# Layer 2's windows: another order of ScalarE's instructions, and other clearing at an image's beginning

## The chip, the cores and the metric

The kernel runs on one core of one Trainium2 chip. The metric is device time in microseconds (us) of one execution, told as the median of several runs. Engines are named as the profile names them: PE is TensorE (matrix products and transposes), DVE is VectorE, ACT is ScalarE, POOL is GpSimd, SP is SyncE, which here only issues transfers (DMAs). DVE and ACT can read PSUM, the memory that PE writes; POOL works on SBUF alone. Each engine runs its own instructions in order and waits on semaphores for those of others.

## The reference, cut to what matters

Four layers follow each other on a batch of 4 images of 192 channels and 64 x 64 pixels in float32. Layer 0 is a deformable convolution with channel attention and an MLP, layer 1 a non-local block, layer 2 attention in overlapping windows with a gated MLP, layer 3 a depthwise convolution with weights computed from the image. The change is in layer 2's attention:

```python
y = _conv1x1(_ln_c(x, n1g, n1b), qkv_w, qkv_b)
cols = _unfold(y, WS, STRIDE, PAD)          # windows of 8 x 8, 6 apart, image padded by 3 zeros
...
q = win[:, :, :HEADS] * temp[None, None]
k = win[:, :, HEADS:2 * HEADS]
v = win[:, :, 2 * HEADS:]
attn = jnp.einsum('blhic,blhjc->blhij', q, k)
attn = attn + bias[None, None]
e = jnp.exp(attn - jnp.max(attn, axis=-1, keepdims=True))
s = jnp.sum(e, axis=-1, keepdims=True)
s_img = _reverse(s, H, W)                   # overlapping windows are added up
o = jnp.einsum('blhij,blhjc->blhic', e, v)
o_img = _reverse(o, H, W).reshape(B, HEADS, ch, H, W)
out = (o_img / s_img[:, :, None]).reshape(B, C, H, W)
```

There are 11 x 11 windows an image and 6 heads of 32 channels. `_ln_c` is a layer norm over the channels of each pixel. The padding makes rows and columns of zeros around the projected image.

## The kernel before, in words

The whole kernel is one program that works image by image. After layer 1 of image b has written its output to the DRAM tensor `x_flat` (tile `xd`, L1050), the function `windows(b, ...)` (from L1095) makes the divided attention output `oi` of that image; `rest` then does the remainder of layers 2 and 3.

**Rows.** `windows` walks over 11 rows of windows (`wr`). For each row it projects a strip of 6 image rows (4 in the last), which are the rows that this row of windows adds to those it shares with the row before. Its work on a row `wr` is woven with the preparation of the next ones:

- `load` (L1118, L1119) brings a strip of `x_flat` into one of two tiles `xr`, in two DMAs: 128 channels, and 64 channels into the lower half of a second block whose upper half is zero.
- `norm_steps` (L1163 to L1179) is the layer norm, as a generator that can be stopped after a step: the squares on ACT (L1163, step SQUARE); the means on PE (tile `pv`, L1170), a square on ACT (L435), a difference and a maximum with zero on DVE (L436, L437), then a logarithm and an exponential on ACT (L398, L399, step INVERSE) for the inverse root; spreading it on PE (`pb`, L427) and scaling the strip on DVE (`xz`, L1179).
- `project_rows(wr, t)` (L1203) makes queries and keys of a strip in three parts t, in a PSUM tile of tag "a", which ACT copies out: t = 0 into `qs` (L1212), t = 1 into `ks` (L1209), t = 2 in halves into both (L1212, L1216). `qs` and `ks` are padded tiles, two sets of them used in turn; `shared` (L1191, POOL) copies the rows that two rows of windows share from one set to the other.
- `values` (L1231, L1235) projects the values in two parts through tag "a" and DVE, and SP writes them to the DRAM tensor `values_dram` (L1243); `fetch` (L1253) reads them back by windows with 16 DMAs on SP into `vw`.
- `queries` (L1264 to L1266) gathers the windows' queries into `qw` on POOL.

**Groups.** The 11 windows of a row are worked on in three groups `g` of four, four and three. `scores` (L1279) makes the scores of a group in the one PSUM tile `s`, and DVE adds the bias (L1285); `lowered` takes the maximum (L1295) and subtracts it (L1296), both on DVE; `exponentials` (L1300) is one ACT instruction of 128 x 768; `summed` (L1306, L1310) makes the sums on DVE. A group has two pairs of windows. `turned` transposes a pair's exponentials on PE (tile `t`, tag "a", L1325) and ACT copies them into `et` (L1329, two copies, one where the pair has only one window). `outputs` multiplies them with the values (L1345) and gathers the sums (L1353) in the PSUM tile `o`; `collect` (L1363, L1364, ACT) copies that out once a row. `inverses` (L1384, L1385, ACT) makes 1/sum of the row before by logarithm and exponential, and `finish` spreads it on PE (`rb`, tag "a", L1390) and multiplies on DVE into `oi` (L1391), in two halves.

**What sets the order.** This stage is written under `tc.manual_schedule()`: each engine gets its instructions in the order of the program text, from L1400 on. PE's order in a full row is, for g = 0: scores of g = 1, t, o, qk (t = 0), v, t, o, qk (t = 2), v; for g = 1: scores of g = 2, t, o, qk (t = 1), t, o, pv; for g = 2: scores of the next row's g = 0, t, o, rb, pb, t, o, rb. The exponentials of the next group are asked for after both pairs of the group and, in g = 1, after the norm's INVERSE step:

```python
                        if wr + 2 < NWIN and g == 1:
                            norm(wr + 2, INVERSE)
                        if nxt[0] < NWIN:
                            ex = exponentials(*nxt, sc)
```

Tag "a" has two PSUM buffers, handed out in turn, for t, qk, v and rb alike: each tile waits until the one two before it has been read. DVE's order in g = 2 is: bias sum of the next row, sums L1306, maximum, subtraction, first `oi`, `xz`, second `oi`.

**An image's beginning.** POOL clears the upper halves of both `xr` (L1124), issues the first two loads (four DMAs), clears the four tiles `qs` and `ks` whole (L1136, 128 x 1224 each), three tiles `et` (L1141) and two tiles `rs` (L1154); for image 0 also a tile `blank` (L1145), from which six DMAs on POOL's queue write the zero border of `values_dram` (L1147 to L1150). The order of text is: square of the first norm, `keep_warm` (matmuls whose result nobody reads, L788), the load of ACT's table for logarithms and exponentials (`table(LN_EXP)`, L393), the rest of the norm, the three projections, queries, values, second norm, fetch, and then the first scores.

`constants` (L261) holds one more line of the change: a copy of a small PSUM tile `wide` (128 x 52), once in the program.

Of the kernel before, what the change touches and what calls it, by code (L numbers as in the profile page):

```python
# [10 lines left out]
F32 = mybir.dt.float32  # L11
# [7 lines left out]
B, C, H, W = 4, 192, 64, 64  # L19
# [5 lines left out]
M, Q = 128, 64  # L25
# [31 lines left out]
NWIN = 11  # L57
# [24 lines left out]
def conv_seq_kernel(ctx: ExitStack, tc: tile.TileContext, a, out: bass.AP):  # L82
    nc = tc.nc
# [102 lines left out]
    def constants():  # L186
# [59 lines left out]
        with pool_of(name="wideps", bufs=1, space=PSUM) as pp:  # L246
            n = sum(n for name, n in _V96 if name in _WIDE)
            wide = const([M, 2, n], "wide")
            p = pp.tile([M, 2, n], F32, tag="p", name="p_wide")
            at = 0  # L250
            for name, n in _V96:
                if name in _WIDE:
                    cols = slice(at, at + n)
                    at += n
                    for to, of, k in (
                        (p[0:P, 0, cols], slice(0, P), 0), (p[P:M, 0, cols], slice(0, M - P), 1),
                        (p[0:Q, 1, cols], slice(M - P, P), 1), (p[Q:M, 1, cols], slice(M - P, P), 1),
                    ):
                        nc.tensor.matmul(to, lhsT=ident[:P, of], rhs=V[name][:, k, :], start=True, stop=True)
                    VW[name] = wide[:, :, cols]  # L260
            nc.vector.tensor_copy(wide, p)  # L261
        yield
        fc1_dram, fc1_bias = folded("fc1", V["l0_g2"], V["l0_b2"], V["l0_bfc1"])
        yield
# [113 lines left out]

    xn_flat = [dram.tile([C, XNW], F32, tag=f"xnd{i}", name=f"xnd{i}") for i in range(2)]
    x_flat = [dram.tile([C, HW], F32, tag=f"xd{i}", name=f"xd{i}") for i in range(2)]  # L380
    values_dram = dram.tile([SW, STRIDE * (NWIN + 1), C], F32, tag="values", name="values")
    xn_drams, x_drams = ([t.rearrange("(k p) n -> p k n", p=P) for t in ts] for ts in (xn_flat, x_flat))

    in_order = []
# [707 lines left out]
                beside(None)  # L1092


    def windows(b, oi, load_image):  # L1095


        inside = slice(PAD, PAD + W)
        with ExitStack() as s:
# [14 lines left out]
            def load(wr, by=nc.sync):  # L1114
                n, at = strip(wr)
                t = given[wr] = xrs[wr % 2]
                lo, hi = split(t, n)
                by.dma_start(out=lo, in_=x_flat[b % 2][0:M, at : at + n])  # L1118
                by.dma_start(out=hi[half(0)], in_=x_flat[b % 2][M:C, at : at + n])  # L1119

            xrs = []
            for j in range(2):
                xr = s1.tile([M, 2, STRIDE * W], F32, tag=f"xr{j}", name=f"xr{j}_{b}")
                nc.gpsimd.memset(xr[half(1), 1, :], 0.0)  # L1124
                xrs.append(xr)

            load(0, nc.gpsimd)
            load(1, nc.gpsimd)


            sets = []
            for j in range(2):
                qs = s1.tile([M, 2, WS + 1, SW], F32, tag=f"qs{j}", name=f"qs{j}_{b}")
                ks = s1.tile([M, 2, WS + 1, SW], F32, tag=f"ks{j}", name=f"ks{j}_{b}")
                for t in (qs, ks):
                    nc.gpsimd.memset(t, 0.0)  # L1136
                sets.append((qs, ks))
            ets = []
            for j in range(3):
                et = s1.tile([128, 3, 2, WS, WS + STRIDE], F32, tag=f"et{j}", name=f"et{j}_{b}")  # L1140
# [2 lines left out]
            if b == 0:  # L1143
                blank = s1.tile([128, 3 * C], F32, tag="blank", name="blank")
                nc.gpsimd.memset(blank, 0.0)  # L1145
                for r in (0, 1, 2, SW - 1):
                    nc.gpsimd.dma_start(out=values_dram[r, 0:SW], in_=blank[0:SW, 0:C])  # L1147
                inner = values_dram[PAD : PAD + H]
                nc.gpsimd.dma_start(out=inner[:, 0:PAD, :], in_=blank[0:H].rearrange("p (w c) -> p w c", c=C))
                nc.gpsimd.dma_start(out=inner[:, PAD + W, :], in_=blank[0:H, 0:C])  # L1150
            rss = []
            for j in range(2):
                rs = s1.tile([128, 512], F32, tag=f"rs{j}", name=f"rs{j}_{b}")
# [27 lines left out]
            def norm(wr, upto=None):  # L1181

                if wr not in norms:
                    norms[wr] = norm_steps(wr)
                links(norms[wr], upto)

            def shared(wr, i):

                to, of = sets[wr % 2][i], sets[1 - wr % 2][i]
                if wr > 0:  # L1190
                    nc.gpsimd.tensor_copy(to[:, :, 0:PAD, :], of[:, :, STRIDE : STRIDE + PAD, :])  # L1191
                end = PAD + strip(wr)[0] // W
                if end < WS + 1:
                    nc.gpsimd.memset(to[:, :, end : WS + 1, :], 0.0)
# [204 lines left out]
            groups = -(-NWIN // WG)  # L1399
            with tc.manual_schedule():  # L1400
                warm = ps2.tile([128, 512], F32, tag="a", name=f"warm_{b}")[:, 0:384]
                norm(0, SQUARE)
                keep_warm(warm, 2)
                in_order.append(None)
                table(LN_EXP)
                norm(0, VARIANCE)
                keep_warm(warm, 2)
                norm(0)
                keep_warm(warm, 1)
                for t in range(3):  # L1410
                    project_rows(0, t)
                    if t == 0:
                        norm(1, SQUARE)
                queries(0)
                norm(1, VARIANCE)
                values(0, 0)
                values(0, 1)
                norm(1)
                fetch(0)
                load(2)  # L1420
                ex, top = scores(0, 0)
                lowered(0, 0, ex, top)
                exponentials(0, 0, ex)
                due = None
                for wr in range(NWIN):
                    for g in range(groups):
                        nxt = (wr, g + 1) if g + 1 < groups else (wr + 1, 0)
                        if nxt[0] < NWIN:
                            sc, top = scores(*nxt)
                        sums = summed(wr, g, ex)  # L1430
                        if nxt[0] < NWIN and (g > 0 or wr + 1 == NWIN):
                            lowered(*nxt, sc, top)
                        if wr + 3 < NWIN and g == 1:
                            load(wr + 3)
                        for pair in range(WG // 2):
                            ops = turned(wr, g, pair, (ex, sums))
                            if due is not None:
                                outputs(*due)
                                if g == 0 and pair == 0:
                                    collect(wr - 1)  # L1440
                            due = ops
                            if wr + 1 < NWIN:
                                if g == 0:
                                    project_rows(wr + 1, 2 * pair)
                                    values(wr + 1, pair)
                                if g == 1 and pair == 0:
                                    project_rows(wr + 1, 1)
                                if g == 0 and pair == 0:
                                    lowered(*nxt, sc, top)
                            if wr == 0 and g == 0 and pair == 0:  # L1450
                                norm(2, SQUARE)
                            if wr > 0 and g == 1 and pair == 0:
                                inverses(wr - 1)
                            if wr > 0 and g == 2:
                                finish(wr - 1, pair)
                            if wr + 2 < NWIN and g == 2 and pair == 0:
                                norm(wr + 2)
                        if wr + 2 < NWIN and g == 1:
                            norm(wr + 2, INVERSE)
                        if nxt[0] < NWIN:  # L1460
                            ex = exponentials(*nxt, sc)
                        if wr + 3 < NWIN and g == 2:
                            norm(wr + 3, SQUARE)
                        if wr + 1 < NWIN:
                            if g == 0:
                                shared(wr + 1, 0)
                                queries(wr + 1)
                            if g == 1:
                                shared(wr + 1, 1)
                                fetch(wr + 1)  # L1470
                    if wr == 1:
                        load_image()
                outputs(*due)
                collect(NWIN - 1)
                inverses(NWIN - 1)
                keep_warm(ps2.tile([128, 512], F32, tag="a", name=f"warm2_{b}")[:, 0:384], 4)
                for h in range(2):
                    finish(NWIN - 1, h)
                in_order.pop()
# [35 lines left out]
    def half(h):  # L1515
        return slice(Q * h, Q * h + Q)
# [697 lines left out]
```

## Time and profile before

| | |
|---|---|
| median of 21 runs | 6435.1 us (6414.39 to 6451.02) |
| the profiled execution's own time | 6434.07 us |
| span of its profile | 6432.3 us |
| mean granted clock of PE | 0.946 |
| PE busy | 5833.2 us (91%) |
| DVE busy | 4645.4 us (72%) |
| ACT busy | 3720.7 us (58%) |
| POOL busy | 1982.5 us (31%) |

All times are of one profiled execution, in us from the span's start. Lines of a timeline give start, duration, engine, line (L and the line number of the kernel), the operation, the tile that it writes and those that it reads (written<-read), shapes, and in square brackets how long the engine was idle just before and what ended that. Lines of the chain of waits give start, duration and the piece of work; "issue" is time in which an engine waited for nothing that the profile shows. Lines of stretches give from:to, length, then the busy time and number of instructions of PE, PE's weight loads, DVE, ACT and POOL, then the granted clock of PE as a share of full speed, the busy share of the DMA engines and what they moved in GB/s.

### The profile page before, as it was taken

The numbers are of one execution on the slowest core, as the hardware profiler recorded it, in microseconds if no ns is written. First come the engines' busy times: TensorE is split into PE (matmuls) and PEld (weight loads), VectorE is DVE, ScalarE is ACT, GpSimd is POOL, SyncE is SP. The second block draws the span as 40 slices with busy tenths as digits, with TensorE's granted clock in tenths as the row PEclk, the third lists the DMA queues.
The fourth block names the chain that finished last, engine by engine and source line by source line (L and its number), as shares of the span: only waits on it lengthen the run. The fifth ranks groups of instructions, "written<-read, shape, count | busy, mean of one in ns | idle before, by whom it ended". The sixth has DMA issues, their size and how long they took to land.

```text
span 6432.3 us, 105494 instructions
## 1 busy us (share of the span) xinstructions
PE 5833.2 (91%) x39860; PEld 4021.9 (63%) x39860; DVE 4645.4 (72%) x6899; ACT 3720.7 (58%) x6288; POOL 1982.5 (31%) x1989
## 2 busy tenths in 40 slices
PE   8887999998879899999888899999888989998897
PEld 4555688886544468887554458888654457775443
DVE  3764189985677659996676849998567867766667
ACT  3764378874545358885654438887455536545542
POOL 2764067751100037772110007775110000001100
PEclk8889999999889899999999999999988999998898
DMA  6986267762110266773210047775221020002100
GB/s 180 294 298 184 71 191 225 224 189 61 46 45 16 62 187 212 231 220 91 78 48 26 19 129 229 223 223 177 62 51 34 16 64 10 13 15 70 28 8 22
DMA packets 385632, 735.33 MB, mean 114 GB/s; under 512 B 67757, under 2 KB 272189, under 8 KB 384358
## 3 DMA queue, kind: packets, MB, share of 16 engines
q0 software_dynamic: 93264, 455.82, 22.0%
q1 hardware_dynamic: 291030, 271.99, 15.6%
q8 instruction: 316, 5.18, 0.3%
q14 instruction: 190, 1.56, 0.1%
q10 hardware_dynamic: 832, 0.79, 0.0%
HBM read 635.04 MB, written 91.86 MB: 113 GB/s over the span
## 4 chain that ended last, share of the span: by engine, by line
PE 63%; DVE 19%; ACT 8%; DMA 4%; issue 4%; SPq 1%; POOL 1%; DVEq 0%; ACTq 0%; POOLq 0%
PE y L1076 11%; PE s L1008 10%; PE h L685 7%; PE qk L1203 3%; DVE ha L1507 2%; PE h L1699 2%; PE o L913 2%; PE po L573 2%; DMA ring<-table,idx 2%; DVE ga L1507 2%; PE t L1325 2%; DVE gate L1507 1%; PE o L1345 1%; PE rb L1390 1%; DVE row L674 1%
## 5 line engine op out<-in xcount | busy, mean ns | idle before, releaser
L667 POOL DMA_INDIRECT ring<-table,idx x1152 | 1659.6, 1441 | 967.8 <-DVE row L674 175.6
L1008 PE MATMUL s<-ths,ph 96*128 96x256 f32 x4096 | 982.5, 381 | 6.9 <-ACT sc L1010 4.6
L1008 PEld LDWEIGHTS s<-ths,ph 96*128 96x128 f32 x4096 | 777.0, 191 | 130.6 <-ACT sc L1010 6.2
L673 ACT ACTIVATE row<-ring,pos 128x384 f32<-128x384 f32 x1152 | 672.5, 608 | 243.1 <-DVE xo L678 143.7
L674 DVE SCALAR_TENSOR_TENSOR row<-ring,fr,row 128x384 f32<-128x384 f32 x1152 | 674.9, 614 | 114.6 <-ACT row L673 109.5
L1076 PE MATMUL y<-sc,gx 128*97 128x256 f32 x3008 | 716.4, 379 | 0.0
L1076 PEld LDWEIGHTS y<-sc,gx 128*97 128x97 f32 x3008 | 489.3, 164 | 127.5 <-issue 5.1
L677 ACT ACTIVATE xo<-row,pos 128x192 f32<-128x192 f32 x1152 | 486.3, 448 | 72.8 <-PE h L685 34.6
L678 DVE SCALAR_TENSOR_TENSOR xo<-row,fr,xo 128x192 f32<-128x192 f32 x1152 | 448.2, 414 | 45.1 <-ACT xo L677 42.6
L1010 ACT COPY sc<-s 128x1024 f32<-128x1024 f32 x376 | 377.3, 1004 | 157.4 <-PE s L1008 154.5
L1073 DVE TENSOR_TENSOR sc<-sc,mbs 128x1024 f32<-128x1024 f32 x376 | 453.9, 1220 | 19.9 <-ACT mbs L1034 19.8
L1015 DVE TENSOR_TENSOR top<-top,sc 128x1024 f32<-128x1024 f32 x282 | 344.6, 1222 | 128.1 <-ACT sc L1010 128.0
L1074 ACT ACTIVATE sc<-sc 128x1024 f32<-128x1024 f32 x376 | 393.3, 1053 | 75.1 <-DVE sc L1073 72.0
L685 PE MATMUL h<-ti,xo 128*128 128x192 f32 x2304 | 434.6, 327 | 0.0
L685 PEld LDWEIGHTS h<-ti,xo 128*128 128x128 f32 x2304 | 388.8, 190 | 28.8 <-issue 8.2
L1329 ACT COPY et<-t 64x384 f32<-64x384 f32 x484 | 231.7, 479 | 254.0 <-PE t L1325 249.0
L1507 DVE SCALAR_TENSOR_TENSOR ga<-gate,v,ga 128x1024 f32<-128x1024 f32 x234 | 300.4, 1284 | 6.7
L685 PE MATMUL h<-kept,xo 128*128 128x192 f32 x960 | 242.7, 385 | 67.8 <-DVE xo L678 57.9
L1325 PE MATMUL t<-ident,ex 128*128 128x128 f32 x792 | 157.1, 313 | 151.3 <-ACT ex L1300 151.3
L1749 POOL COPY gate<-gate 128x192 f32<-128x192 f32 x12 | 4.2, 348 | 902.4 <-ACT gate L1742 902.4
L685 PEld LDWEIGHTS h<-kept,xo 128*128 128x128 f32 x960 | 172.6, 213 | 164.2 <-DVE xo L678 117.8
L890 PE MATMUL h<-d_l0m,fc 128*128 128x256 f32 x768 | 213.0, 420 | 60.4 <-ACT z L1705 22.5
(412 smaller groups left out, 10803.8 us busy)
## 6 DMA issues: line engine op xcount, KB each, us to landing
ti<-table SPq DMA_DIRECT2D x768, 48.0 KB
ring<-table,idx POOLq DMA_INDIRECT x1152
xnd<-xn SPq DMA_DIRECT2D x4, 3270.0 KB
vw<-values SPq DMA_DIRECT2D x352, 36.0 KB
xi<-in_x_dram SPq DMA_DIRECT2D x32, 384.0 KB
xk<-xd SPq DMA_DIRECT2D x32, 384.0 KB
xd<-xc SPq DMA_DIRECT2D x64, 192.0 KB
table<-tt SPq DMA_DIRECT2D x32, 384.0 KB
```

Of the source, the lines that this page charges most:

```text
L667: nc.gpsimd.indirect_dma_start(out=gt.rearrange("p q r c -> p (q r c)"), out_offset=None, in_=corners, in_offset=bass.IndirectOffsetOnAxis ...
L673: nc.scalar.activation(row, gt[:, 0], AF.Copy, scale=pos[:, t, 9 + tap : 10 + tap])
L674: nc.vector.scalar_tensor_tensor(row, gt[:, 1], fr[:, t, 9 + tap : 10 + tap], row, ALU.mult, ALU.add)
L677: nc.scalar.activation(xo[:, j, :], row[:, 0, :], AF.Copy, scale=pos[:, t, tap : tap + 1])
L678: nc.vector.scalar_tensor_tensor(xo[:, j, :], row[:, 1, :], fr[:, t, tap : tap + 1], xo[:, j, :], ALU.mult, ALU.add)
L685: nc.tensor.matmul(acc[m // 2][:, bass.ts(m % 2, C)], lhsT=xo.rearrange("p j c -> p (j c)")[:, bass.ts(m, 128)], rhs=tt, start=t == 0 and ...
L1008: nc.tensor.matmul(p[:, t, :], lhsT=ph[:, bass.ts(G * g + t, 128)], rhs=ths[i], start=True, stop=True)
L1010: nc.scalar.copy(to, p)
L1073: nc.vector.tensor_tensor(ex, ex, mbs[i].unsqueeze(1).to_broadcast([128, G, QN]), ALU.add)
L1074: nc.scalar.activation(ex, ex, AF.Exp)
L1076: nc.tensor.matmul(py, lhsT=gx[:, G * g + t, :], rhs=ex[:, t, :], start=g == 0 and t == 0, stop=g == NG - 1 and t == G - 1,)
L1507: nc.vector.scalar_tensor_tensor(acc[:, b], src(tap, b), w[:, tap : tap + 1], acc[:, b], ALU.mult, ALU.add)
```

## The change

ACT's copy of `wide` in `constants` was DVE's. `values_dram` is allocated when `windows` first runs. At an image's beginning the loads are issued ahead of clearing `xr`; of `qs` and `ks` only the three columns on the left, the column on the right and, in the first set, the three rows on top are cleared; the six DMAs of the border go to SP's queue. `shared` copies the used half of the second block only, in two copies instead of one. In the order of text, the table's load and six calls of `keep_warm` precede the first squares; projection 2 and the queries precede projection 1; the first scores and exponentials precede the values, the fetch and the second norm. In the loop, `exponentials` of the next group is asked for as soon as the second pair's `turned` and `outputs` are: ahead of projection 2's copies in g = 0, and ahead of the norm's INVERSE step in g = 1. In g = 2, and in the last row, ACT's order stays.

```diff
-            nc.vector.tensor_copy(wide, p)
+            nc.scalar.copy(wide, p)
...
+            xrs = cleared([M, 2, STRIDE * W], ("xr0", "xr1"))
             load(0, nc.gpsimd)
             load(1, nc.gpsimd)
-
-
+            for t in xrs:
+                nc.gpsimd.memset(t[half(1), 1, :], 0.0)
             sets = []
             for j in range(2):
-                qs = s1.tile([M, 2, WS + 1, SW], F32, tag=f"qs{j}", name=f"qs{j}_{b}")
-                ks = s1.tile([M, 2, WS + 1, SW], F32, tag=f"ks{j}", name=f"ks{j}_{b}")
-                for t in (qs, ks):
-                    nc.gpsimd.memset(t, 0.0)
-                sets.append((qs, ks))
+                sets.append(cleared([M, 2, WS + 1, SW], (f"qs{j}", f"ks{j}")))
+                for t in sets[j]:
+                    nc.gpsimd.memset(t[:, :, :, 0:PAD], 0.0)
+                    nc.gpsimd.memset(t[:, :, :, PAD + W : SW], 0.0)
+                    if j == 0:
+                        nc.gpsimd.memset(t[:, :, 0:PAD, inside], 0.0)
...
-                    nc.gpsimd.dma_start(out=values_dram[r, 0:SW], in_=blank[0:SW, 0:C])
+                    nc.sync.dma_start(out=values_dram[r, 0:SW], in_=blank[0:SW, 0:C])
...
-                    nc.gpsimd.tensor_copy(to[:, :, 0:PAD, :], of[:, :, STRIDE : STRIDE + PAD, :])
+                    for at in ((slice(0, M), 0), (half(0), 1)):
+                        nc.gpsimd.tensor_copy(to[at + (slice(0, PAD),)], of[at + (slice(STRIDE, STRIDE + PAD),)])
...
+                in_order.append(None)
+                table(LN_EXP)
+                keep_warm(warm, 6)
                 norm(0, SQUARE)
                 keep_warm(warm, 2)
-                in_order.append(None)
-                table(LN_EXP)
                 norm(0, VARIANCE)
                 keep_warm(warm, 2)
                 norm(0)
                 keep_warm(warm, 1)
-                for t in range(3):
+                for t in (0, 2):
                     project_rows(0, t)
-                    if t == 0:
-                        norm(1, SQUARE)
                 queries(0)
-                norm(1, VARIANCE)
-                values(0, 0)
-                values(0, 1)
-                norm(1)
-                fetch(0)
-                load(2)
+                project_rows(0, 1)
+                norm(1, SQUARE)
                 ex, top = scores(0, 0)
                 lowered(0, 0, ex, top)
                 exponentials(0, 0, ex)
+                values(0, 0)
+                values(0, 1)
+                fetch(0)
+                norm(1, VARIANCE)
+                norm(1)
+                load(2)
...
                             due = ops
+                            if pair == 1 and nxt[0] < NWIN:
+                                ex = exponentials(*nxt, sc)
                             if wr + 1 < NWIN:
                                 if g == 0:
                                     project_rows(wr + 1, 2 * pair)
...
-                        if nxt[0] < NWIN:
-                            ex = exponentials(*nxt, sc)
```

`cleared` only allocates the named tiles.

More of the change, by code (lines that the diff above doesn't have):

```diff
@@ L380, in conv_seq_kernel @@
     x_flat = [dram.tile([C, HW], F32, tag=f"xd{i}", name=f"xd{i}") for i in range(2)]
-    values_dram = dram.tile([SW, STRIDE * (NWIN + 1), C], F32, tag="values", name="values")
     xn_drams, x_drams = ([t.rearrange("(k p) n -> p k n", p=P) for t in ts] for ts in (xn_flat, x_flat))
@@ L1092, in layer1 @@
                 beside(None)
+    frames = []
     def windows(b, oi, load_image):
+        if not frames:
+            frames.append(dram.tile([SW, STRIDE * (NWIN + 1), C], F32, tag="values", name="values"))
+        values_dram = frames[0]
         inside = slice(PAD, PAD + W)
@@ L1119, in load, with cleared @@
                 by.dma_start(out=hi[half(0)], in_=x_flat[b % 2][M:C, at : at + n])
[L1121 to L1125, printed above, removed]
+            def cleared(shape, names):
+                return [s1.tile(shape, F32, tag=n, name=f"{n}_{b}") for n in names]
+            xrs = cleared([M, 2, STRIDE * W], ("xr0", "xr1"))
             load(0, nc.gpsimd)
             load(1, nc.gpsimd)
+            for t in xrs:
+                nc.gpsimd.memset(t[half(1), 1, :], 0.0)
             sets = []
             for j in range(2):
-                qs = s1.tile([M, 2, WS + 1, SW], F32, tag=f"qs{j}", name=f"qs{j}_{b}")
-                ks = s1.tile([M, 2, WS + 1, SW], F32, tag=f"ks{j}", name=f"ks{j}_{b}")
-                for t in (qs, ks):
-                    nc.gpsimd.memset(t, 0.0)
-                sets.append((qs, ks))
+                sets.append(cleared([M, 2, WS + 1, SW], (f"qs{j}", f"ks{j}")))
[4 more added lines that the diff above has]
+                        nc.gpsimd.memset(t[:, :, 0:PAD, inside], 0.0)
             ets = []
@@ L1146, in windows @@
                 for r in (0, 1, 2, SW - 1):
-                    nc.gpsimd.dma_start(out=values_dram[r, 0:SW], in_=blank[0:SW, 0:C])
+                    nc.sync.dma_start(out=values_dram[r, 0:SW], in_=blank[0:SW, 0:C])
                 inner = values_dram[PAD : PAD + H]
-                nc.gpsimd.dma_start(out=inner[:, 0:PAD, :], in_=blank[0:H].rearrange("p (w c) -> p w c", c=C))
-                nc.gpsimd.dma_start(out=inner[:, PAD + W, :], in_=blank[0:H, 0:C])
+                nc.sync.dma_start(out=inner[:, 0:PAD, :], in_=blank[0:H].rearrange("p (w c) -> p w c", c=C))
+                nc.sync.dma_start(out=inner[:, PAD + W, :], in_=blank[0:H, 0:C])
             rss = []
```

## Prediction

> **What bounds the kernel.** The page's chain that ended last gives PE 63% of the span and no line over 11%, so the kernel is many stages and the change is priced in its own one: the windows of layer 2, run four times. From the timeline, the stage from the first scaled norm (L1179, 1519.97) to the last division (L1391, 1776.3) takes 256 us for image 0; with 249, 257 and 260 us for the others it is 1022 us, 16% of the span. A stage is 11 rows of windows. The distances between the copies L1363, one a row, average 22.93, 21.81, 22.93 and 23.37 us by image over rows 1 to 7: **22.76 us a row**. I read the chain of waits within one row next:
>
> ```profile
> 1604.75 0.67 ACT qs L1212
> 1605.45 0.58 ACT ks L1216
> 1606.03 0.74 ACT ex L1300
> 1606.77 0.04 issue
> 1606.81 0.55 PE t L1325 x3
> ...
> 1611.59 0.48 ACT et L1329
> ...
> 1612.09 0.26 ACT r_l2n L435
> ...
> 1613.60 0.74 ACT ex L1300
> 1614.34 0.04 issue
> 1614.38 0.55 PE t L1325 x3
> ```
>
> (L1279 is the scores, L1300 their exponential, L1325 the transposes t.) Twice a row PE waits for an exponential (L1300) that stands on ScalarE behind other work: behind two copies (group 0), and behind the norm's square, logarithm and exponential (L435 to L399, group 1). The second wait is the longer, and does more than idle; the stretches around it show the granted clock (the 1.00, 0.66, 0.50 ahead of the DMA share):
>
> ```profile
> 1611.00:1613.00 2.00, 0.59 (x48) 0.45 (x38) 0.59 (x3) 1.38 (x5) 0.00 (x0) 1.00 0.50 93
> 1613.00:1615.00 2.00, 0.62 (x12) 0.45 (x16) 1.38 (x2) 1.33 (x4) 0.00 (x0) 1.00 0.49 91
> 1615.00:1617.00 2.00, 2.00 (x21) 1.25 (x16) 1.93 (x4) 0.93 (x2) 0.00 (x0) 0.66 0.04 12
> 1617.00:1619.00 2.00, 2.00 (x14) 1.67 (x17) 1.43 (x3) 0.00 (x0) 0.00 (x0) 0.50 0.04 8
> ```
>
> After the wait PE runs at half clock. Cut into steps of 0.1 us, every fall and rise of the clock in these stages lies on a grid of 3.41 us. Of the grid's slots at full clock, those with PE busy below 0.47 were all followed by a slow slot, those from 0.47 to 0.56 in 8 of 12 cases, those above in none of the windows' stages. A slow row takes 7.94 us from group 2's first t to the next row's first (1684.47 to 1692.41), one at full clock 5.18 (1593.30 to 1598.48): 2.76 us for two slow slots, **1.4 each**. Rows that kept the clock take 21.0.
>
> The Trainium skill ("TensorE: Matmul & The Clock Gate", What's actually happening) has the same window of 3413 ns, but lets the clock fall only after an idle window. By that rule a wait of 2.8 us would cost no clock, a row could give back only its waits, and the rows' term below would be 32 x 0.36 = +12. The stretches above decide against it.
>
> **Group 0, exponential ahead of the copies.** Its input (L1296) ends at 1604.91, the copies et ahead of it at 1603.86, so it runs 1604.93 to 1605.77 instead of from 1606.03. But behind it stand now the copies qs (0.67) and ks (0.58): they end at 1607.05 instead of 1606.03. Tag "a" has two buffers, handed out in the order t, qk, v, t, qk, v, t: the last of these, group 1's first, takes the buffer of the second qk and must wait for both copies. It starts at 1607.09, not 1606.81: **+0.28**. GpSimd's queries wait for the same copy; they end at 1606.5 now, 1607.6 then, and the scores that need them start at 1610.8: hidden.
>
> **Group 1, exponential ahead of the root.** Here is the rest of a row that kept its clock:
>
> ```profile
> 1593.28 0.95 DVE L1306 TENSOR_REDUCE eh<-ex 128x12 f32<-128x768 f32 x1 [0.62 <-ACT ex L1300]
> 1593.30 0.55 PE L1325 MATMUL t<-ident,ex 128*128 128x128 f32 x3 [2.79 <-ACT ex L1300]
> ...
> 1596.23 0.54 DVE L1391 TENSOR_TENSOR oi<-ot,rb 96x384 f32<-96x384 f32 x1
> ...
> 1596.94 0.89 PE L1390 MATMUL rb<-rs,headsel 128*96 128x384 f32 x2
> ```
>
> In it the copies et end at 1590.99; with the 0.28 at 1591.27. The exponential (0.83) ends at 1592.12 and t starts at 1592.16: **1.14 earlier**. Square (0.25) now ends at 1592.39 instead of 1591.26. On VectorE its two followers and the next scores' sum L1285 end 1.40 after it (1591.26 to 1592.66), so at 1593.79, and the reduction L1306 starts 0.50 later than now. From there VectorE is full up to L1391: the first division ends at 1597.27, not 1596.77. The second rb (L1390) takes that division's buffer: it starts at 1597.30, not 1596.94. So what was gained on PE is lost again there, and a row at full clock becomes **0.36 longer: 21.4**. PE's waits are then 1.0 (group 0), 2.79 - 1.14 - 0.28 = 1.37 (group 1) and 1.55 (second rb: the o ahead of it end at 1595.75). The largest leaves a slot that holds all of it 0.55 busy, the upper edge of what fell. Such a slot comes in (3.41-1.55)/3.41 = 0.54 of rows; I let a good third of them fall: one row in five, 1.4 each, 0.3 a row.
>
> Rows 1 to 8 have both moves: 32 rows x (22.76 - 21.4 - 0.3) = 32 x 1.1 = **-35 us**. Bounds: none falls, -44; half fall, 32 x (1.36 - 0.7) = -21. Rows 0, 9 and 10 at nothing: row 9 has no norm, and its exponential already follows et.
>
> **An image's beginning**, shown for image 1:
>
> ```profile
> 3036.68 0.77 POOL L1124 MEMSET xr<- 64x384 f32 x2 [86.77 <-DMA xd<-xc]
> 3041.77 0.84 ACT L1163 ACTIVATE sq_l2n<-xr 128x768 f32<-128x768 f32 x1 [13.14 <-DMA xr<-xd]
> 3042.63 1.28 ACT L393 ACT_TABLE_LOAD   x1
> 3044.50 2.28 DVE L437 TENSOR_SCALAR r_l2n<-r_l2n 128x96 f32<-128x96 f32 x1
> 3045.73 0.98 POOL L1154 MEMSET rs<- 128x512 f32 x2
> 3046.81 0.37 ACT L398 ACTIVATE r_l2n<-r_l2n,eps 128x96 f32<-128x96 f32 x1 [2.64 <-DVE r_l2n L437]
> ```
>
> L437 takes 0.21 us in the rows; here 2.28, and in images 0, 2 and 3 3.27, 3.39 and 5.21. Each time it ends 0.07 after GpSimd's run of memsets does (3046.78 against 3046.71). So the memsets' end sets the beginning. The four of 128x1224, 1.06 apart, are 4.24; in their place come ten small ones. From 0.41 (384 elements) and 1.12 (1224) a memset is 0.09 + 0.85 ns an element: eight of 18 or 54 elements near 0.12, two of 384 at 0.41, 1.8 with no overlap, 1.2 with the overlap of 0.06 each. Saving 2.4 to 3.0; I take **2.7**. The loads ahead of L1124 bring the data 0.77 earlier and the table (1.28) goes under the wait for them, so L437's input is ready at 3043.4, ahead of the memsets' new end at 3044.0: neither is late. Image 0 has one rs memset more ahead of L437, and its DMAs move to SP (six, up to 0.6 each, while SP has nothing until 1529.7): 2.3. In image 3 keep_warm(6), twelve matmuls of 0.32 to 0.64, stands before pv (5797.02) with nothing to wait for: 3.9 to 7.7 later, against 2.7 from the memsets; between -1.1 and +2.7, taken at 0. In the other images PE idles 6.6 us there. Sum -2.3 - 2.7 - 2.7 = **-7.7**; bounds -12 and -4.
>
> The Trainium skill ("SBUF — State Buffer", SBUF: two separate sides) calls the port that VectorE and GpSimd share a lock held for the whole instruction, after which the other goes. By that L437 would wait for one memset, at most 1.12, and only the earlier loads and the hidden table would count here, an estimate of -3; in this trace it waited for the whole run, 5.21 in image 3.
>
> **After the first norm** scores now precede the values. Before, the first o comes 20.4 us after xz (1541.33 - 1520.92), and the fetch's issues end 16.3 after it. Now the value sums follow the subtraction, 10.3 after xz, plus 1.3 and 6.05 of issues: 17.6, and landing took about 2.4 for xr: 20.0. Second norm and t stand on PE as before. Taken at nothing, -1.5 to +1.5 an image.
>
> **Nothing else pays.** The copy of wide (0.21, once, at 118 us) moves to ScalarE: -0.2 to +0.7. The split copy in shared adds about 0.2 on GpSimd, idle 3 us around it. The place of the values table changes no instruction.
>
> Sum: -35 - 7.7 = -43 on the profiled execution's 6434.07 (span 6432.3): **6391 us**. The median of 21 runs is 6435.1, so no correction. Its own range: -44 - 12 - 6 gives 6372; -21 - 4 + 7 gives 6416.
>
> **Rivals.** *The clock falls once a row all the same* (the wait at rb is the new trigger): 21.4 + 1.4 = 22.8 is what a row takes now, only the beginning's -8 is left: 6426. For it: 0.55 is an edge, and the clock falls in 8 of 12 slots just under it. Against: the three slots of 0.56 to 0.59 held.
> *Slower*: the wait for the first division before the second rb reaches 1.7 us (busy 0.50), from which slots mostly fall; the slow slots then lie on the next row's projections, which end late, and a second slot is slow: 21.4 + 2.8 = 24.2, 32 x 1.4 - 8 = +38: 6472. It needs 0.15 us more than I worked out.
> *Much faster*: VectorE is not late and PE keeps the 1.14: 21.0 - 1.1 = 19.9, 32 x 2.9 + 8 = -100: 6334. Against it stands the order on VectorE, both sums ahead of the division.
>
> **Chances**: forecast 0.62, once a row 0.15, slower 0.13, much faster 0.10. The range takes in the forecast's own and the first rival, and part of the way to the fast one: 6362 to 6438. About 0.2% (13 us) is what a measurement tells from no change: faster 0.72, same 0.15, slower 0.13.
>
> **What would show it.** The t after group 1's exponential waits about 1.4, not 2.8; the t's buffer, not the exponential, ends the wait in group 0 (ScalarE ks L1216); the second rb waits 1.5 for L1391; clock 1.00 through most rows, rows near 21.4; L437 ending with shorter memsets, 2.7 earlier against the xr loads' start. Wrong if rows still show 0.50 after each wait, or if rb waits over 1.7.

## The result: 2.2 per cent slower

The changed kernel takes 6571.8 us (median of 8 runs, 6566.4 to 6580.9), the kernel before 6434.2: a ratio of 1.0216 (95% interval 1.0205 to 1.0228). The forecast was 6391, its range ended at 6438. The profiled execution of the changed kernel takes 6588.5 us, with a span of 6586.7.

| | before | after |
|---|---|---|
| span, us | 6432.3 | 6586.7 |
| ACT busy | 3720.7, 6288 instructions | 3953.0, 6468 instructions |
| granted clock of PE, mean | 0.946 | 0.931 |
| windows' stage, first square to last copy `ot`, sum of four images | 1040.7 | 1176.3 |
| a row (between copies `ot`), mean of rows 1 to 7 | 22.76 | 25.57 |

The stage is 135.6 us longer, of 154.4 in the span. ACT is busy 232.3 us more, though the change adds nothing to ACT but one small copy. The groups of instructions tell what it is (line, engine, operation and number; busy time and mean ns of one; idle time ahead of them). Lines are numbered by each run's own kernel: in the changed one the lines of the windows' stage stand 5 or 6 further down (the exponential L1300 is L1306, the transposes L1325 are L1331), the norm's root one further up.

```profile
L397 ACT ACT_TABLE_LOAD x44 | 56.5, 1283 | 0.8
L398 ACT ACT_TABLE_LOAD x44 | 56.5, 1283 | 0.8
L1390 ACT ACT_TABLE_LOAD x44 | 56.5, 1283 | 0.8
L1391 ACT ACT_TABLE_LOAD x44 | 56.5, 1283 | 0.8
L392 ACT ACT_TABLE_LOAD x41 | 52.6, 1283 | 1.4 <-PEq L2211 0.7
L390 ACT ACT_TABLE_LOAD x40 | 51.3, 1283 | 0.7
```

L397 and L398 are the logarithm and the exponential of the norm's root, L1390 and L1391 those of the sums' inverse. Before, none of these four lines had a load. They are 176 x 1.283 = 225.8 us, and three more loads stand at L390. L392 is `table(LN_EXP)`, the request that the change moved. The first instructions on ACT are these:

```profile
0.73 1.28 ACT L392 ACT_TABLE_LOAD   x1 [0.73 <-PEq L2211]
2.02 1.28 ACT L390 ACT_TABLE_LOAD   x1
...
8.46 1.28 ACT L392 ACT_TABLE_LOAD   x1
9.75 1.28 ACT L390 ACT_TABLE_LOAD   x1
11.04 1.06 ACT L451 ACTIVATE sq_l<-d_l 96x1024 f32<-96x1024 f32 x1
```

Four requests for the logarithm's table and four for Gelu's, one of each for every image, are carried out at the start of the program, 1500 us and more ahead of their place in the text. A load reads and writes no tile. Where it is the first ACT instruction of a part under a manual schedule, nothing in that part stands ahead of it, and the scheduler that orders the whole program put it in front of everything (inferred from where the requests stand; runs 1 and 2 move nothing but this line). When the windows' stage begins, layer 1 has left another table in place, and the function `table`, which leaves out a request for the set that it asked for last, believes the right one is there. So the program was given a load wherever a function needed a table, and it loads for each function on its own: one for the logarithm, another for the exponential after it, and so on all along the row.

This is the chain of waits in one row after (start, duration, piece), where before it had the projection's copies and the exponential:

```profile
1618.02 0.58 ACT ks L1215
1618.61 0.02 issue
1618.62 1.28 ACT L1390
1619.91 0.01 issue
1619.92 0.52 ACT rs L1390
1620.44 0.02 issue
1620.46 1.28 ACT L1391
1621.74 0.01 issue
1621.75 0.52 ACT rs L1391
...
1623.27 0.84 ACT ex L1306
1624.11 0.03 issue
1624.14 0.25 ACT r_l2n L434
1624.39 0.02 issue
1624.40 1.28 ACT L397
```

The pieces without a tile's name are the loads; the fourth comes at 1626.09. TensorE's transposes of this row wait for the exponential behind them 3.95 us, where they waited 2.79, and the clock falls for the longer wait (columns as in the prediction's stretches):

```profile
1624.17 0.90 PE L1331 MATMUL t<-ident,ex 128*128 128x128 f32 x3 [3.95 <-ACT ex L1306]
```

```profile
1622.00:1624.00 2.00, 0.00 (x0) 0.00 (x0) 0.00 (x0) 1.95 (x4) 0.00 (x0) 0.84 0.34 92
1624.00:1626.00 2.00, 1.83 (x20) 1.18 (x20) 1.55 (x4) 1.95 (x4) 0.00 (x0) 0.50 0.08 21
1626.00:1628.00 2.00, 1.77 (x3) 0.57 (x4) 1.93 (x4) 1.97 (x4) 0.00 (x0) 0.50 0.00 0
```

PE does nothing for 2 us while ACT is busy for 1.95 of them, and then runs at half clock for some 9 us (1.00 again from 1634).

The Trainium skill ("ScalarE: Activation LUTs", Table sets: the hidden batching unit) counts one load for a logarithm and an exponential, since one set holds both. Here that holds only where the program asks for that set by name; left to the automatic loads, a pair cost two.

**The theory** is then: the change is worth what its other parts give, less the price of 176 loads in a row's way. **The rival**: the loads lie in idle time of ACT, and the new order of a row is what costs, as the prediction's slower case had it.

### The profile page after: what moved, and what is told of

The parts are those of the page before. It is cut to its first block, busy times and chain, and to the rows that moved or that the text cites. A ratio compares the mean times of both kernels' runs of the same rounds, so it can differ in the third digit from the quotient of the medians.

```text
span 6586.7 us, 105980 instructions
## 1 busy us (share of the span) xinstructions
PE 5940.0 (90%) x39908; PEld 4074.7 (62%) x39908; DVE 4638.0 (70%) x6898; ACT 3953.0 (60%) x6468; POOL 1974.7 (30%) x2087
## 4 chain that ended last, share of the span: by engine, by line
PE 61%; DVE 18%; ACT 10%; DMA 5%; issue 4%; SPq 1%; POOL 1%; DVEq 0%; ACTq 0%; POOLq 0%
PE y L1075 11%; PE s L1007 10%; PE h L684 7%; PE qk L1209 2%; PE h L1706 2%; DVE ha L1514 2%; PE o L912 2%; PE po L572 2%; DMA ring<-table,idx 2%; DVE ga L1514 2%; DVE gate L1514 1%; PE h L889 1%; DVE row L673 1%; DVE top L1014 1%; PE pb_l2n L426 1%
## 5 line engine op out<-in xcount | busy, mean ns | idle before, releaser
L1072 DVE TENSOR_TENSOR sc<-sc,mbs 128x1024 f32<-128x1024 f32 x376 | 453.9, 1219 | 20.0 <-ACT mbs L1033 19.9
L1331 PE MATMUL t<-ident,ex 128*128 128x128 f32 x792 | 166.1, 328 | 170.6 <-ACT ex L1306 170.6
```

What stands on the lines that cost most here:

```text
L1072: nc.vector.tensor_tensor(ex, ex, mbs[i].unsqueeze(1).to_broadcast([128, G, QN]), ALU.add)
```

## The experiments

Expectations in us stand for a kernel before of 6434 us. The runs were made on three chips; on two of them the kernel before takes 6598.5 and 6604.5 us (the stages ahead of the windows take longer there: the first square of the windows' stage comes at 1610.4 us in run 4, at 1502.6 in run 11), on the third 6434.4. So ratios to the kernel before on the same chip are what is compared. A ratio is estimated from all runs of a kernel; the ratio of the two medians can differ from it by 0.001.

**1. The changed kernel with the table back.** One line moves.

```diff
                 in_order.append(None)
-                table(LN_EXP)
                 keep_warm(warm, 6)
                 norm(0, SQUARE)
+                table(LN_EXP)
                 keep_warm(warm, 2)
```

> The changed kernel with one line moved: the table of Ln and Exp is asked for behind the first square again, not as the first ScalarE instruction of the patches' stage. Everything else of the change stays. Theory (the table loads): in the changed kernel's trace the request stands at the program's beginning (8 loads there, 1 before), and 176 loads of 1.283 us stand ahead of each Ln and Exp of the stage; without them rows go from 25.6 us to what the prediction gave for the rest of the change, 21.4 to 21.8, and the whole to 6391 to 6400 us. Rival (the order of a row is what costs: the first division late before the second rb, or the exponential ahead of the copies): the loads lie in ScalarE's idle time, rows stay above 24 and the whole above 6470.

Measured: 6481.0 us, a ratio of **0.9819** (0.9796 to 0.9842). The 176 loads are gone, rows take 19.56 in the mean, most of them 19.32 to 19.34. The rival falls. But the gain is more than twice what the theory gave for the rest of the change.

**2. The kernel before with only the table moved.**

```diff
-                norm(0, SQUARE)
-                keep_warm(warm, 2)
                 in_order.append(None)
                 table(LN_EXP)
+                norm(0, SQUARE)
+                keep_warm(warm, 2)
                 norm(0, VARIANCE)
```

> The kernel before with only the request for the table moved ahead of the first square; no exponential, load or memset is moved. Theory (the table loads): the same 176 loads appear, and with them 4 x 1.283 us of ScalarE in each row; rows go from 22.8 to 25.5 or more (here the exponentials stand behind the loads too, so up to 27), the whole to 6560 to 6640 us. Rival (the order of a row): within 10 us of 6434.

Measured: 6804.2 us, **1.0311** (1.0282 to 1.0339), rows of 27.43. The same 44 loads stand at each of the four lines. This one moved line alone costs more than the whole change did (1.0216).

**3. The kernel before with only the loop's exponentials moved.**

```diff
                             due = ops
+                            if pair == 1 and nxt[0] < NWIN:
+                                ex = exponentials(*nxt, sc)
...
-                        if nxt[0] < NWIN:
-                            ex = exponentials(*nxt, sc)
```

> The kernel before with only the loop's exponentials asked for ahead of the projection's copies and the norm's root; the table's place and the image's beginning are as before. The prediction's term for the rows: -35 us (bounds -44 and -21), 6399 us, rows of 21.4 with one in five 1.4 longer. Rival 1 (the clock still falls once a row): 6434. Rival 2 (the first division is late before the second rb): 6472. Rival 3 (TensorE keeps all of the 1.14): 6340.

Measured: 6486.4 us, **0.9817** (0.9797 to 0.9837), rows of 19.33. That is beyond even the prediction's "much faster". This is where its step on the second `rb` and the one on `t`'s buffer can be looked at, in one row of this kernel:

```profile
1732.06 0.67 ACT L1212 ACTIVATE qs<-qk,qkb,wide 64x384 f32<-64x384 f32 x1
1732.27 0.55 PE L1325 MATMUL t<-ident,ex 128*128 128x128 f32 x3
...
1732.76 0.59 ACT L1216 ACTIVATE ks<-qk,qkb 64x384 f32<-64x384 f32 x1
```

```profile
1742.21 0.89 PE L1390 MATMUL rb<-rs,headsel 128*96 128x384 f32 x2
...
1743.05 0.54 DVE L1391 TENSOR_TENSOR oi<-ot,rb 96x384 f32<-96x384 f32 x1
```

The transposes `t` start at 1732.27, while the copies `qs` and `ks` run until 1733.35: they don't wait for the second `qk`'s buffer. The second `rb` starts at 1742.21, before the first division begins: it doesn't wait for that buffer either. Neither of the two PE lines has an idle time in brackets. The two buffers of tag "a" are not handed out in strict turn, as this document's description of the kernel and the prediction had it: with the second `qk`'s still being read, `t` can only have the bank of the last `v`, which VectorE had read by 1732.00. For `rb` the trace of before showed it already. PE's weight load ahead of the second `rb` (PEld) waits for the copy `et`, which reads the `t` between the two `rb`, there as in run 3:

```profile
1596.94 0.24 PEld L1390 LDWEIGHTS rb<-rs,headsel 128*96 128x96 f32 x2 [0.29 <-ACT et L1329]
```

```profile
1742.21 0.24 PEld L1390 LDWEIGHTS rb<-rs,headsel 128*96 128x96 f32 x2 [0.30 <-ACT et L1329]
```

`rb` reads nothing of `et`, so this is the wait for a buffer, and the buffer is that `t`'s, not the first `rb`'s.

The waits that are left in that row are 1.40 us at group 1's `t` and 0.23 at the next row's:

```profile
1738.58 0.55 PE L1325 MATMUL t<-ident,ex 128*128 128x128 f32 x3 [1.40 <-ACT ex L1300]
...
1744.06 0.55 PE L1325 MATMUL t<-ident,ex 128*128 128x128 f32 x3 [0.23 <-ACT ex L1300]
```

**4. The beginning alone**: the kernel of run 1 with the loop's exponentials at their old place (run 3's diff, reversed).

> The changed kernel with the table back behind the first square and with the loop's exponentials back behind the copies and the root: what is left is the beginning of an image (loads first, only edges cleared, scores ahead of the values, six more matmuls to keep the clock), the split copy in shared and the copy of wide on ScalarE. The prediction's term: -8 us (bounds -12 and -4, and -1.5 to +1.5 an image for the new order): 6426 us. Rival (the beginning loses, by image 3's keep_warm of six or by the order after the first norm): 6440 to 6450.

Measured: 6618.2 us, 1.0019 (0.9999 to 1.0038): no gain.

**5 and 6. The exponential early in one group alone**, in the kernel before.

```diff
+                            if g == 1 and pair == 1 and nxt[0] < NWIN:
+                                ex = exponentials(*nxt, sc)
...
-                        if nxt[0] < NWIN:
+                        if nxt[0] < NWIN and g != 1:
                             ex = exponentials(*nxt, sc)
```

(and the same with 0 for 1.)

> The kernel before with the early exponential in group 1 alone (ahead of the norm's square, logarithm and exponential); groups 0 and 2 as before. Theory from the run with all three (no buffer is waited for; TensorE keeps what ScalarE gives): the wait of 2.79 us becomes 2.79 - 1.14 = 1.65, the wait of 0.73 in group 0 stays, rows that keep the clock take 19.9, some fall (a slot that holds 1.65 is 0.52 busy), 20.4 in the mean: 36 rows x 2.2 = -80 us, a ratio of 0.988. The prediction's step (VectorE late, second rb behind the first division): rows of 21.1 or more, a ratio of 0.994 or above.

> The kernel before with the early exponential in group 0 alone (ahead of the copies qs and ks). Theory (the transposes take the buffer of v, not of the second qk): the wait of 0.73 us is gone and nothing takes its place; group 1's wait and the fall of the clock stay: rows 0.7 shorter, 36 x 0.7 = -25 us, a ratio of 0.996. The prediction's step (the transposes wait for ks): 0.28 a row longer, +10 us, 1.0015.

Measured: group 1 alone 6521.0 us, **0.9873** (0.9848 to 0.9899), rows of 19.97 to 20.10 but for the first of each image (21.4); PE waits 0.72, 1.39 and 0.24 in a row. Group 0 alone 6559.6, **0.9923** (0.9898 to 0.9947); rows that keep the clock take 20.43, others up to 23.1. The row at full clock was 21.08: 1.10 shorter by the one, 0.65 by the other, and 1.75 by both (19.33). The terms add up. The wait of 0.72 went without another coming; of the 1.40 that group 1's wait lost, 0.24 came back at the next row's `t`. Run 6 gained twice what was expected (0.996), since more rows kept the clock: 13 of 28, against 5 of 28 in the trace of before, though the wait of 2.79 is still there.

**7 and 8. Further along the same line**: from run 1, group 1's exponential also ahead of the second pair's copies `et`; and then the norm's square and what follows it behind the next scores' sum and reduction on VectorE.

```diff
+                            if pair == 1 and g == 1 and nxt[0] < NWIN:
+                                following = exponentials(*nxt, sc)
                             ops = turned(wr, g, pair, (ex, sums))
...
-                        if wr + 2 < NWIN and g == 1:
-                            norm(wr + 2, INVERSE)
```

(run 8 alone has the last two lines, and asks for this norm in g = 2, behind `summed`.)

> The changed kernel with the table back in its place and, in group 1, the exponential one step earlier: ahead of the copies et of the second pair (0.97 us) too. Its input is there 0.4 us before those copies start. Theory: the last wait of a row, 1.40 us, becomes 0.4; rows of 18.3 in place of 19.3, -36 us, a ratio to before of 0.976. Rival (VectorE stands behind the norm's square, whose place doesn't move, and the next exponential comes from there): the wait comes back in front of the next row's first transposes, 0.23 us now and 1.2 then; a ratio of 0.981 to 0.983.

> As the run before, and the norm's square with what follows it (L434 to L398) is asked for behind the next scores' sum and reduction on VectorE, not ahead of them. Theory: VectorE no longer stands 2.6 us behind the square; its next exponential's input comes 1.5 earlier, the spread norm (pb) 0.2 later: rows of 17.8 to 18.2, a ratio to before of 0.973 to 0.976. Rival (the rest of a row is TensorE's own work already, or pb's later input is waited for): no faster than the run before it.

Measured: run 7 6483.7 us, 0.9813 (0.9789 to 0.9838), rows of 19.2. The rival's ratio came out, its place only in part: group 1's wait is down from 1.40 to 0.41, but the norm's square ends where it did, VectorE stands behind it, and the wait is spread over later places (0.32 for `et`, 0.31 in place of 1.2 for the next exponential). Run 8 moves that, and gives 6469.5 us, **0.9790** (0.9764 to 0.9815), rows of 18.83; the expected 17.8 to 18.2 was too low. The two waits left are 0.27 and 0.31. It is the fastest of these kernels, though its interval overlaps those of runs 1, 3 and 7.

**9 and 10. Two loads a row in the kernel of run 1**, at one of the two places each: `table(GELU)` and `table(LN_EXP)` ahead of the sums' logarithm, or ahead of the norm's.

> The changed kernel with the table back in its place, and two table loads (Gelu's, then that of Ln and Exp again) put ahead of the sums' logarithm in each row: 44 x 2 loads, half of the changed kernel's 176, at one of its two places. Here ScalarE comes to group 1's exponential through them. Theory (a load ahead of the exponential that TensorE waits for is paid in full): rows of 19.3 + 2.57 = 21.9, and more where the longer wait lets the clock fall, as in the changed kernel; 40 x 2.6 = +104 us and up, a ratio to before of 0.998 to 1.010. Rival (ScalarE has the room: it idles 0.65 ahead of ks): +1.3 a row, 0.990.

> As the run before, with the two loads ahead of the norm's logarithm in place of the sums': behind group 1's exponential, in front of the copies et that follow. Theory: the transposes of group 2 have their copies late by 2.57, and the norm spread by TensorE (pb) by the same; TensorE's work from there to pb (1.7 us) covers part: +1.5 to +2.6 a row, 60 to 104 us, a ratio to before of 0.991 to 1.0. The two runs together, less twice the run without extra loads, should give what the changed kernel has over it (4.0 per cent); rival (loads aren't what costs in the changed kernel): less than half of that.

Measured: ahead of the sums' logarithm 6497.4 us, **1.0102** (1.0087 to 1.0118), rows of 23.9; ahead of the norm's 6390.8 us, **0.9933** (0.9920 to 0.9947), rows of 20.98 that mostly keep the clock. Over run 1 that is 2.83 and 1.14 per cent, 3.97 together; the four loads of the changed kernel cost 3.9 (next run). So loads that are put back by themselves cost what the changed kernel lost, and nothing else is needed to explain it. The first place is dearer, since the exponential that TensorE waits for stands behind it:

```profile
1650.84 1.28 ACT L390 ACT_TABLE_LOAD   x1
1652.13 1.28 ACT L392 ACT_TABLE_LOAD   x1
1653.42 0.52 ACT L1392 ACTIVATE rs<-ot 6x384 f32<-6x384 f32 x1
...
1655.49 0.84 ACT L1306 ACTIVATE ex<-ex 128x768 f32<-128x768 f32 x1
...
1656.39 0.90 PE L1331 MATMUL t<-ident,ex 128*128 128x128 f32 x3 [3.96 <-ACT ex L1306]
```

PE waits 3.96 us there, 2.57 more than run 1's 1.39, and the clock falls on top: 24.0 against 19.33 is 4.7. At the second place the wait is 1.39 as in run 1, and 1.69 at the spread norm (`pb`): 1.65 a row, and the clock holds in most rows.

```profile
1607.06 0.55 PE L1333 MATMUL t<-ident,ex 128*128 128x128 f32 x3 [1.39 <-ACT ex L1308]
...
1610.63 1.13 PE L428 MATMUL pb_l2n<-r_l2n,spread 128*128 128x96 f32 x8 [1.69 <-ACT r_l2n L400]
```

**11 and 12. The two kernels unchanged**, on the chip of runs 9 and 10.

> The kernel before, unchanged, for its trace on the chip of this call: rows of 21.1 where the clock is kept and 22.5 to 23.9 where it falls, as on the first chip. What differs from the first chip lies outside the patches' stage.

> The changed kernel, unchanged, beside the runs of this call. Theory (ScalarE's 4 x 1.283 us a row is paid in full, and the clock falls for the longer wait): rows of 25.1 to 26.1 as on the first chip, a ratio of 1.020 to 1.024, so that the table's place is worth 1.022 - 0.982 = 4.0 per cent, some 260 us, and 226 of them the loads themselves. Rival (the first chip was special): a ratio below 1.01.

Measured: the changed kernel 6572.4 us, 1.0206 (1.0183 to 1.0229), rows of 25.54; the kernel before has rows of 21.08 to 23.88.

## Why the prediction was wrong, point by point

**The failed step is in the beginning: "the table (1.28) goes under the wait for them".** It took the load to run where the text has it, and priced its move at nothing. The load went to the start of the program, and the stage got 176 in its place. From 0.9819 to 1.0206 that is 3.9 per cent of 6434, about 249 us. The loads themselves take 226; the clock falls too, to 0.80 to 0.86 in the mean of a row, where it is 1.00 in 23 of 28 rows of run 1. How the 249 divide between the two was not measured. None of the rivals had this mechanism; the slower one (6472, by the second `rb`) was on the right side for a wrong reason, and too small. The trace of before could have told it. ACT's first instruction there was this, with ACT's first work 8.3 us after its end:

```profile
0.73 1.28 ACT L391 ACT_TABLE_LOAD   x1 [0.73 <-PEq L2204]
10.28 1.06 ACT L452 ACTIVATE sq_l<-d_l 96x1024 f32<-96x1024 f32 x1 [8.26 <-DVE d_l L449]
```

```profile
L391 ACT ACT_TABLE_LOAD x37 | 47.5, 1283 | 1.4 <-PEq L2204 0.7
L1705 ACT ACT_TABLE_LOAD x4 | 5.1, 1283 | 5.3 <-DVE ha L1650 5.3
```

L391 is `table(GELU)`. The layer needs Gelu's table at L1705, whose part of the program begins with that request on ACT, and yet four automatic loads, one an image, stand at L1705, and a request for Gelu's table is carried out at 0.73. So a request that comes first in its part had already been taken to the program's start: four alike, which became one (37 loads at L391, where the changed kernel has 40). The change gave the windows' request the same place.

**Rows: "-35 us", measured -118** (run 3, 0.0183 of 6434). The mechanism, a wait that ends earlier and a clock that falls less, was right; the size was not, by two sub-steps with one root. The prediction had all of the rows' gain from the clock: a row at full clock was to be 0.36 longer, and it is 1.75 shorter (21.08 to 19.33). "+0.28" for group 0: measured -0.65, the wait of 0.73 is gone (run 6). "The second rb takes that division's buffer", a wait of 1.55 that gives the gain back: it does not, and no such wait is there (run 3). Both took tag "a" for two buffers in strict turn. What was worked out from durations alone held: group 1's wait was to be 1.37 and is 1.40. The expected delay on VectorE ("the reduction L1306 starts 0.50 later") fell with the 0.28: in run 3 L1306 starts 13.81 after the row's first copy, before 14.30 in a row that kept the clock. "Much faster" had rows of 19.9; they are 19.33, since group 0's 0.73 is in neither of its terms.

**The clock.** "The largest leaves a slot that holds all of it 0.55 busy", one row in five was let fall. The largest wait was not that one, 1.55 at `rb`, but group 1's, mostly 1.39, which leaves a slot 0.59 busy. Of 28 rows of run 3, one fell (20.68), all others took 19.01 to 19.34; in run 1, with the same loop, five of 28 fell (20.65 to 21.28). So one row in five is what run 1 had, by waits other than the prediction's: the share came out by luck. With 2.79 (run 6) rows still took up to 23.1. The edge that the prediction read from the trace holds roughly, and not as a sharp one: between the first and the last copy `ot` of an image, slots with PE busy 0.57 to 0.64 were followed by a slow one in none of 6 cases in the trace of before, but in 4 of 61 in runs 1, 3 and 5. Its "8 of 12" for slots of 0.47 to 0.56 are 6 of 11 when the trace's clock records are counted over the four stages.

**The beginning: -7.7, measured nothing in the whole time** (run 4). Its local steps held in part. In the changed kernel the vector instruction ahead of the logarithm (L437 before) still ends with GpSimd's memsets, which are shorter:

```profile
3066.79 0.57 POOL L1123 DMA_DIRECT2D xr<-xd  x1 [87.79 <-DMA xd<-xc]
...
3070.03 0.43 POOL L1142 MEMSET qs<- 128x384 f32 x1
...
3072.68 1.31 DVE L436 TENSOR_SCALAR r_l2n<-r_l2n 128x96 f32<-128x96 f32 x1
3072.94 0.98 POOL L1159 MEMSET rs<- 128x512 f32 x2
...
3074.41 1.28 ACT L398 ACT_TABLE_LOAD   x1
```

It ends at 3073.99, 0.07 after the memsets, and 7.20 after the first load's issue; before, 9.38 (3046.78 - 3037.40): 2.2 earlier, against 2.7 expected. "The loads ahead of L1124 bring the data 0.77 earlier" did not show: the first square came 12.4 to 13.5 us after layer 1's last copy `yn` before, and 12.8 to 13.3 in run 4, in images 0 to 2. From that `yn` to the first copy `ot`, run 4 is 6.3 us shorter in the four images than run 11 (image 3 alone 3.1, where nothing was expected; the two runs are of different chips). But from there on its rows take 19.9 us more in sum (877.7 against 857.9): more of them are slow, many near 23.9, which is seven of the clock's slots of 3.41. Why an earlier beginning leads to more slow rows was not tried; that it shifts the rows against the clock's grid is argued, not shown. With the exponentials early, run 1 against run 3, the beginning makes no difference that can be told (0.9819 against 0.9817).

**"After the first norm", the copy of `wide` and the split copy**, all taken at nothing, were not measured apart; run 4 holds them.

## What to carry to other kernels

An instruction without operands may have no place of its own: ask what in the program keeps it where the text has it, and look in the trace whether others of its kind stand where their text does. When the price of a new wait is worked out, it must be known which buffer is taken, not how many there are. And one change can hold a large gain and a larger loss: here one line's place hid 1.8 per cent, and only the parts run alone showed both.

## What the runs showed of the hardware

- A table load takes 1.283 us each time, and the next instruction on ACT starts 0.01 us after it. The Trainium skill ("ScalarE: Activation LUTs", What ACT_TABLE_LOAD costs) gives the same 1283 ns and adds a drain of about 1380 ns for each switch. No such drain stands in these rows: 1.28 us of load, then the logarithm, in the chain above. By the page's sum 176 switches would be an estimate of 468 us; about 249 were lost, part of that to the clock.
- A load's price depends on who waits behind it: 1.65 us a row for two loads behind the exponential, 4.7 for two ahead of it, 2.1 of these beyond the loads' own time.
- Slow rows gather near seven slots of the clock's grid (7 x 3.41 = 23.9; 23.6 to 24.3 us in 58 of 84 rows of runs 4, 9 and 11): once such a row has come, most of those after it have the same length.
